# Moving two of three transposes of each matrix set from TensorE to VectorE and DRAM, for the first 20 of 32 images

## The chip, the cores and the metric

The kernel runs on one core of a Trainium2 chip. The metric is the time on the device in microseconds (us) from the start to the end of one execution. Everything is float32. The engines are TensorE (PE, with its weight loads shown apart as PEld), VectorE (DVE), ScalarE (ACT), GpSimd (POOL) and SyncE (SP), which here only issues DMAs.

## The reference, cut to what matters

The input x is 32 images of 32 channels of 128x128. Layer 0 normalizes the image in 16 groups of two channels, takes each channel's matrix X to five steps of a coupled Newton iteration for a matrix square root, and adds the result to x. Layer 1 normalizes again, takes a two-dimensional Fourier transform, keeps 64x32 modes, multiplies them by weights over the channels, transforms back and adds.

```python
def _L0_conv_ref(A):                      # A: normalized x, 1024 matrices of 128x128
    normA = jnp.sqrt(jnp.sum(A2 * A2, axis=(1, 2)))
    Y = A2 / normA[:, None, None]
    Z = I
    for _ in range(5):
        T = 0.5 * (3.0 * I - jnp.matmul(Z, Y))
        Y = jnp.matmul(Y, T)
        Z = jnp.matmul(T, Z)
    return Y * jnp.sqrt(normA)[:, None, None]

x = x + _L0_conv_ref(_gn(x))
x = x + _L1_conv_ref(_gn(x), weights1, weights2)
```

The change touches only layer 0.

## The kernel before, in words

**Sets.** The unit of work of layer 0 is a set: four channels of one image, held as a tile of 128 partitions by 4 x 128 numbers (256 KB). There are 256 sets, eight to an image. The five iterations are rewritten as polynomials: `newton` (L305) runs two `quartic` blocks (L294) and a few more products. A "group" below is one `products` (L245) or one `transposed` (L251): four 128x128 products, or four 128x128 transposes by a product with the identity, into one PSUM bank. A set takes ten groups of products and three groups of transposes: one in each `quartic` (L299, of `v`), and one of `m` (L313).

**A quartic.** PE multiplies `mb` and `m`; DVE adds `m` to the PSUM result and writes `v` (L297, through `plus`, L239). PE transposes `v`, and DVE adds `r` to it and writes `w` (L299). PE multiplies `v` and `w`, and DVE adds a multiple of the identity and writes `q` (L301). `r` is `mb` plus a multiple of the identity, made by POOL at L291 and L315. The other products are copied from PSUM by ACT (`taken`, L231).

**Staging.** `fetch` (L259) loads a set twice through ACT's DMA queue, as it is (`b`) and transposed (`xt`). `staged` (L265) normalizes both: four POOL operations make `m` from `xt` (L272), four ACT operations make `mb` in place (L282), and POOL makes `r`. The means and scales come from `prep` (L160), which loads the image once more (`xs`, L167) and runs `bn_stats` on DVE.

**What sets the order.** Every engine runs its instructions in the order in which the program issues them. The program is a loop of rounds (L783). In each round it goes over the lanes (four, `LANES`); a lane holds one `newton` generator and makes one step of it, up to the next `yield`. A quartic has three steps and the whole `newton` thirteen calls, the last of which only ends it, so the lane is then free. Lanes start three rounds apart, so that at any time four sets are at different steps, and what a step needs was issued one round before. Between the lanes one step each is made of `preps`, `specs`, `posts`, `prods` and `backs`: the statistics of the next image, the forward transform (`settle` L333, which stores the finished `xt` to `mid` through SP's queue, lets POOL fold it and DVE take `bn_stats` of it; `forward`, `spectrum`), the products over channels, and the way back (`inverse` L636). The images are in three parts of 21, 8 and 3 (`GROUPS`); products and way back of the first part start after its 21st image and run beside the Newton steps of the images after it.

**Memory.** The pool `sets` (L109) holds the sets' tiles, with a fixed number of buffers for each name (three of `v`, `w`, `q`; four of `r`, `x`, `y`; ten of `xt`; six of `b`). The pools `modes` and `inv` (L106 and L107), used only from the 21st image on, are held from the start.

Of the kernel before, what the change touches and what calls it, by code (L numbers as in the profile page):

```python
# [21 lines left out]
F32 = mybir.dt.float32  # L25
AF = mybir.ActivationFunctionType
# [6 lines left out]
B = 32  # L33
C = 32
G = 16
LANES = 4
GROUPS = (21, 8, 3)


# [2 lines left out]
QD = 39 / QA  # L42
EYE = 36 / 16
QS = EYE / QD
NB = 8
EPS = 1e-5
K = 64
# [12 lines left out]
def conv_preact_kernel(  # L60
# [42 lines left out]
    up = ctx.enter_context(tc.tile_pool(name="up", bufs=1))  # L103
    sp = ctx.enter_context(tc.tile_pool(name="sp", bufs=1))
    small = ctx.enter_context(tc.tile_pool(name="small", bufs=1))
    modes = ctx.enter_context(tc.tile_pool(name="modes", bufs=1))  # L106
    inv = ctx.enter_context(tc.tile_pool(name="inv", bufs=1))  # L107
    phase = ctx.enter_context(ExitStack())
    sets = phase.enter_context(tc.tile_pool(name="sets", bufs=1))  # L109
    ps8 = ctx.enter_context(tc.tile_pool(name="ps8", bufs=8, space=PSUM))  # L110

    diags = [modes.tile([P, 2048], F32, name=f"diag{i}") for i in range(2)]
    plain = [modes.tile([P, 1024], F32, name=f"plain{i}") for i in range(2)]

    tail = False

# [40 lines left out]
    def prep(b, made):  # L160

        st = small.tile([P, C, 6], F32, tag="a_st", name=f"a_st{b}", bufs=2)
        tiles = []

        def load(i):
            t = stp.tile([P, 4, P], F32, tag="xs", name=f"xs{b}_{i}")
            kept(nc.scalar.dma_start(out=t, in_=xt_in[b, :, 4 * i : 4 * i + 4, :]))  # L167
            tiles.append(t)

        for i in range(3):  # L170
            load(i)
        yield
        for i in range(C // 4):
            for c in range(4):
                nc.vector.bn_stats(st[:, 4 * i + c, :], tiles[i][:, c, :])  # L175
            yield
            if i + 3 < C // 4:
                load(i + 3)
        _, nm, d = yield from moments(st, "a")
        q = small.tile([P, C], F32, tag="a_qs", name=f"a_qs{b}")  # L180
        nc.vector.tensor_reduce(
            q, d.rearrange("p g (c e) -> p (g c) e", e=2), AX.X, ALU.add
        )
        yield
        pq = bank()[:, 0, 0:C]
        nc.tensor.matmul(pq, avg_mean, q, start=True, stop=True)

        v = small.tile([P, C + G], F32, tag="a_v", name=f"a_v{b}")
        nc.vector.tensor_scalar_mul(v[:, 0:C], pq, -512 / (P * P))
        yield  # L190
        vg = small.tile([P, G], F32, tag="a_vg", name=f"a_vg{b}")
        nc.vector.tensor_reduce(
            vg, v[:, 0:C].rearrange("p (g c) -> p g c", c=2), AX.X, ALU.add
        )
        nc.vector.tensor_scalar(v[:, C:], vg, 0.5, EPS, ALU.mult, ALU.add)
        s = root(v, C + G, "a_r")
        inv = small.tile([P, C + G], F32, tag="a_inv", name=f"a_inv{b}")
        nc.vector.reciprocal(inv, s)
        yield

        sc = small.tile([P, C], F32, tag="a_sc", name=f"a_sc{b}", bufs=2)
        nc.vector.tensor_scalar_mul(sc, inv[:, 0:C], 1.0 / P)
        n = small.tile([P, G, 2], F32, tag="a_n", name=f"a_n{b}")
        nc.vector.tensor_tensor(  # L204
            n,
            s[:, 0:C].rearrange("p (g c) -> p g c", c=2),
            inv[:, C:, None].to_broadcast([P, G, 2]),
            ALU.mult,
        )
        nn = small.tile([P, C], F32, tag="a_nn", name=f"a_nn{b}")  # L210
        nc.vector.tensor_scalar_mul(
            nn, n.rearrange("p g c -> p (g c)"), P * (1.5 / EYE) ** 2
        )
        sn = root(nn, C, "a_t")

        scr = small.tile([P, C], F32, tag="a_scr", name=f"a_scr{b}", bufs=2)
        nc.vector.tensor_scalar_mul(scr, sc, QR * QS)
        off = small.tile([P, G, 2], F32, tag="a_off", name=f"a_off{b}", bufs=2)
        nc.vector.tensor_tensor(
            off,  # L220
            scr.rearrange("p (g c) -> p g c", c=2),
            nm[:, :, None].to_broadcast([P, G, 2]),
            ALU.mult,
        )
        made[b] = (nm, sc, sn, scr, off.rearrange("p g c -> p (g c)"))
        yield

    def four(tag, bufs):
        return sets.tile([P, 4, P], F32, tag=tag, name=tag, bufs=bufs)

    def taken(ps, tag, bufs=4, f=1.0):  # L231
        t = four(tag, bufs)
        if f == 1.0:
            nc.scalar.copy(t, ps)  # L234
        else:
            nc.scalar.mul(t, ps, f)  # L236
        return t

    def plus(ps, f, t, tag, bufs=4):  # L239

        s = four(tag, bufs)
        nc.vector.scalar_tensor_tensor(s, ps, f, t, ALU.mult, ALU.add)  # L242
        return s

    def products(lhsT, rhs):  # L245
        ps = bank()
        for j in range(4):
            nc.tensor.matmul(ps[:, j, :], lhsT[:, j, :], rhs[:, j, :], start=True, stop=True)  # L248
        return ps

    def transposed(t):  # L251
# [5 lines left out]
    raw = {}  # L257

    def fetch(b, g):  # L259
        xt, t = four("xt", 10), four("b", 6)  # L260
        kept(nc.scalar.dma_start(out=t, in_=x[b, :, 4 * g : 4 * g + 4, :]))
        kept(nc.scalar.dma_start(out=xt, in_=xt_in[b, :, 4 * g : 4 * g + 4, :]))
        raw[b, g] = xt, t

    def staged(b, g, nm, sc, sn, scr, off):  # L265

        chans = range(4 * g, 4 * g + 4)
        m = four("x", 4)
        xt, mb = raw.pop((b, g))
        for j, c in enumerate(chans):  # L270
            kept(
                nc.gpsimd.tensor_scalar(  # L272
                    m[:, j, :],
                    xt[:, j, :],
                    nm[:, c // 2 : c // 2 + 1],
                    sc[:, c : c + 1],
                    ALU.add,
                    ALU.mult,
                )
            )  # L280
            kept(
                nc.scalar.activation(  # L282
                    mb[:, j, :],
                    mb[:, j, :],
                    AF.Identity,
                    bias=off[:, c : c + 1],
                    scale=scr[:, c : c + 1],
                )
            )
        r = four("r", 4)  # L290
        nc.gpsimd.tensor_tensor(r, mb, eye, ALU.add)  # L291
        return xt, m, mb, r

    def quartic(m, mb, r):  # L294


        v = plus(products(mb, m), -1 / (QA * QR * QS), m, "v", 3)  # L297
        yield
        w = plus(transposed(v), -QA * QS, r, "w", 3)  # L299
        yield  # L300
        q = plus(products(v, w), -QA / (16 * QS), eye, "q", 3)  # L301
        yield
        return q

    def newton(g, sn, xt, m, mb, r):  # L305


        q = yield from quartic(m, mb, r)
        y = taken(products(q, m), "y")
        yield  # L310
        m = taken(products(q, y), "m", 3)
        yield
        mb = taken(transposed(m), "mb", 2, QR * QS)  # L313
        r = four("r", 4)
        nc.gpsimd.tensor_tensor(r, mb, eye, ALU.add)  # L315
        yield
        q = yield from quartic(m, mb, r)
        pw, py = products(q, m), products(q, y)
        w, y = taken(pw, "t", 3), taken(py, "y4", 2)
        yield  # L320
        t = plus(products(w, q), -0.5 * EYE / 1.5, eye, "t", 3)
        yield
        ps = products(t, y)
        for j in range(4):
            c = 4 * g + j
            nc.vector.scalar_tensor_tensor(  # L326
                xt[:, j, :], ps[:, j, :], sn[:, c : c + 1], xt[:, j, :], ALU.mult, ALU.add
            )
        yield

    folds = {}

    def settle(b, g, st, xt):  # L333

# [7 lines left out]
            )  # L342
        for j in range(4):
            nc.vector.bn_stats(st[:, 4 * g + j, :], xt[:, j, :])
        yield

    def forward(b, q, u):
# [376 lines left out]
    late = []  # L724
    late_wts = []
    lanes = [None] * LANES
    todo = [(b, g) for b in range(B) for g in range(C // 4)]
    fetches = list(todo)
    stages = list(todo)
# [3 lines left out]
    def stage():  # L733

        b, g = stages.pop(0)
        if g == 0:
            while b not in made:
                step(preps)
            if b + 1 < B:
                preps.append(prep(b + 1, made))  # L740
        ready.append(staged(b, g, *made[b]))
        if fetches:
            fetch(*fetches.pop(0))

# [37 lines left out]
    rounds = 0  # L782
    while todo or any(lanes) or posts or specs or prods or backs:  # L783
        tail = not todo and not any(lanes)
        if tail and not posts and not late:

            phase.close()
# [2 lines left out]
                late_wts.append(late[0].tile([P, 2, 4, 4, C], F32, name=f"wt{kk}_late"))  # L790
                nc.gpsimd.dma_start(out=late_wts[-1], in_=wk[kk])
        for i in range(LANES):
            if lanes[i] is None and todo and rounds >= 3 * i:
                b, g = todo.pop(0)
                xt = ready[0][0]
                lanes[i] = (b, g, xt, newton(g, made[b][2], *ready.pop(0)))
                if stages:
                    stage()
            if lanes[i] is not None:
# [79 lines left out]
```

## Time and profile before

The page and the table describe one profiled execution. Engine times are busy times; a busy PE is one with at least one product under way.

| what | us |
|---|---|
| median of 3 runs (3231.84 to 3234.92) | 3232.51 |
| the profiled execution | 3229.76 |
| its span, first to last instruction | 3227.9 |
| PE busy in the span | 3072.5 |
| PE busy in 100 us at 2500 us, inside the second half | 89.54 |
| DVE, POOL, ACT busy in the span | 2316.4, 1767.5, 1467.4 |

The kernel has two halves. Up to about 1940 us there are Newton sets and the forward transform only; after that the way back of earlier images runs beside the Newton sets of later ones, and DMA traffic doubles. The change acts in the first of them, so shares of the whole span say less than those of the stretch from 100 to 1700 us.

### The profile page before, as it was taken

What the parts mean: (1) busy time and instruction counts of PE and PEld (TensorE: products, weight loads), DVE (VectorE), ACT (ScalarE), POOL (GpSimd) and SP (SyncE); (2) the same over time, 40 slices, a digit from 0 to 9 for tenths busy, and PEclk for the clock granted to TensorE, in tenths of its full rate; (3) what the DMA queues carried; (4) which work ended last, traced back from release to release, by engine and by line L of the source; (5) the groups of instructions that cost most, each with busy time, mean ns of one, the idle gap of its engine ahead of it and who ended that gap; (6) DMA issues with size and microseconds to landing.
All of it is one profiled execution on the core that took longest, in us unless ns stands there. A gap on an engine that the chain in (4) does not pass through costs nothing.

```text
span 3227.9 us, 78350 instructions
## 1 busy us (share of the span) xinstructions
PE 3072.5 (95%) x30656; PEld 2949.3 (91%) x30656; DVE 2316.4 (72%) x6408; ACT 1467.4 (45%) x3076; POOL 1767.5 (55%) x2312
## 2 busy tenths in 40 slices
PE   6999999999999999999999999999999899999954
PEld 6999999999999999999999999999899888989854
DVE  6777777777777777777777776578777777756646
ACT  3444444444444444444444444444444444435433
POOL 4555555455555555555555554376667667636642
PEclk9999999999999999999999999999999999999985
DMA  3333333332233333333333236766666676576577
GB/s 125 102 102 99 105 100 101 99 97 94 92 100 102 100 105 102 102 102 102 96 97 95 93 102 212 228 226 203 227 208 226 210 235 225 180 214 210 193 262 251
DMA packets 270722, 478.06 MB, mean 148 GB/s; under 512 B 80912, under 2 KB 90384, under 8 KB 270352
## 3 DMA queue, kind: packets, MB, share of 16 engines
q1 hardware_dynamic: 154864, 253.84, 24.0%
q10 hardware_dynamic: 113472, 211.86, 20.6%
q0 software_dynamic: 2016, 7.34, 0.6%
q8 instruction: 242, 3.96, 0.5%
q14 instruction: 128, 1.05, 0.1%
HBM read 319.06 MB, written 153.88 MB: 147 GB/s over the span
## 4 chain that ended last, share of the span: by engine, by line
PE 85%; DMA 6%; DVE 6%; ACT 1%; issue 1%; POOL 0%; SPq 0%; ACTq 0%; DVEq 0%; POOLq 0%
PE ps L248 67%; PE ps L254 11%; DMA xs<-in_xt 3%; PE ps L358 2%; PE ps L680 2%; DVE yt L697 2%; DMA or<-od 1%; PE ps L492 1%; PE ps L395 1%; PE ps L658 1%; DVE xt L326 1%; DVE a_st L175 1%; PE ps L563 1%; DMA od<-om 0%; DVE q L242 0%
## 5 line engine op out<-in xcount | busy, mean ns | idle before, releaser
L340 POOL TENSOR_TENSOR fold<-xt 128x256 f32<-128x256 f32 x512 | 363.3, 731 | 600.0 <-DVE xt L326 535.7
L291 POOL TENSOR_TENSOR r<-b,eye 128x512 f32<-128x512 f32 x256 | 327.2, 1278 | 638.0 <-issue 613.1
L248 PE MATMUL ps<-w,v 128*128 128x128 f32 x4096 | 550.0, 278 | 5.6 <-DVE w L242 5.5
L248 PE MATMUL ps<-y,q 128*128 128x128 f32 x4096 | 548.1, 277 | 0.3 <-ACT y L234 0.3
L248 PEld LDWEIGHTS ps<-w,v 128*128 128x128 f32 x4096 | 502.2, 193 | 8.3 <-DVE w L242 4.5
L248 PEld LDWEIGHTS ps<-y,q 128*128 128x128 f32 x4096 | 504.1, 194 | 1.3 <-ACT y L234 0.7
L234 ACT COPY y<-ps 128x512 f32<-128x512 f32 x512 | 299.8, 586 | 357.4 <-PE ps L248 356.9
L272 POOL TENSOR_SCALAR x<-xt,a_nm,a_sc 128x128 f32<-128x128 f32 x1024 | 451.9, 456 | 16.8 <-DVE a_n L204 15.8
L282 ACT ACTIVATE b<-b,a_off,a_scr 128x128 f32<-128x128 f32 x1024 | 422.4, 485 | 1.6 <-DMA b<-in_x 1.6
L242 DVE SCALAR_TENSOR_TENSOR w<-ps,r 128x512 f32<-128x512 f32 x512 | 349.9, 685 | 74.8 <-PE ps L254 70.3
L242 DVE SCALAR_TENSOR_TENSOR q<-ps,eye 128x512 f32<-128x512 f32 x512 | 348.5, 682 | 54.1 <-PE ps L248 46.7
L633 POOL TENSOR_TENSOR yt<-yt,d 128x512 f32<-128x512 f32 x236 | 298.1, 1290 | 152.4 <-ACT d L692 138.5
L242 DVE SCALAR_TENSOR_TENSOR v<-ps,m 128x512 f32<-128x512 f32 x256 | 176.4, 689 | 242.5 <-PE ps L248 242.0
L326 DVE SCALAR_TENSOR_TENSOR xt<-ps,a_t_s,xt 128x128 f32<-128x128 f32 x1024 | 289.6, 341 | 84.2 <-PE ps L248 80.8
L315 POOL TENSOR_TENSOR r<-mb,eye 128x512 f32<-128x512 f32 x256 | 326.8, 1276 | 32.8 <-ACT mb L236 32.7
L242 DVE SCALAR_TENSOR_TENSOR v<-ps,x 128x512 f32<-128x512 f32 x256 | 176.6, 690 | 219.5 <-PE ps L248 219.2
L236 ACT ACTIVATE mb<-ps 128x512 f32<-128x512 f32 x256 | 153.1, 598 | 381.4 <-PE ps L254 370.2
L254 PE MATMUL ps<-ident,v 128*128 128x128 f32 x2048 | 311.3, 275 | 7.2 <-DVE v L242 6.9
L248 PE MATMUL ps<-m,q 128*128 128x128 f32 x2048 | 285.5, 283 | 18.7 <-DVE q L242 16.1
L248 PE MATMUL ps<-y,t 128*128 128x128 f32 x2048 | 279.5, 280 | 3.5 <-DVE t L242 3.4
L248 PEld LDWEIGHTS ps<-m,q 128*128 128x128 f32 x2048 | 253.5, 195 | 28.7 <-DVE q L242 16.8
L248 PE MATMUL ps<-x,b 128*128 128x128 f32 x2048 | 273.4, 277 | 3.9 <-POOL x L272 3.9
(117 smaller groups left out, 5212.5 us busy)
## 6 DMA issues: line engine op xcount, KB each, us to landing
b<-in_x ACTq DMA_DIRECT2D x256, 256.0 KB
xt<-in_xt ACTq DMA_DIRECT2D x256, 256.0 KB
xs<-in_xt ACTq DMA_DIRECT2D x256, 256.0 KB
mid<-xt SPq DMA_DIRECT2D x256, 256.0 KB
yt<-mid SPq DMA_DIRECT2D x128, 512.0 KB
out<-yt SPq DMA_DIRECT2D x108, 512.0 KB
ob<-od SPq DMA_DIRECT2D x42, 256.0 KB
out<-yt ACTq DMA_DIRECT2D x20, 512.0 KB
```

The source lines that it names most:

```text
L234: nc.scalar.copy(t, ps)
L236: nc.scalar.mul(t, ps, f)
L242: nc.vector.scalar_tensor_tensor(s, ps, f, t, ALU.mult, ALU.add)
L248: nc.tensor.matmul(ps[:, j, :], lhsT[:, j, :], rhs[:, j, :], start=True, stop=True)
L254: nc.tensor.transpose(ps[:, j, :], t[:, j, :], ident)
L272: nc.gpsimd.tensor_scalar(m[:, j, :], xt[:, j, :], nm[:, c // 2 : c // 2 + 1], sc[:, c : c + 1], ALU.add, ALU.mult,)
L282: nc.scalar.activation(mb[:, j, :], mb[:, j, :], AF.Identity, bias=off[:, c : c + 1], scale=scr[:, c : c + 1],)
L291: nc.gpsimd.tensor_tensor(r, mb, eye, ALU.add)
L315: nc.gpsimd.tensor_tensor(r, mb, eye, ALU.add)
L326: nc.vector.scalar_tensor_tensor(xt[:, j, :], ps[:, j, :], sn[:, c : c + 1], xt[:, j, :], ALU.mult, ALU.add)
L340: nc.gpsimd.tensor_tensor(f[:, :, 64 * half : 64 * half + 64], xt[:, :, 0:64], xt[:, :, 64:128], op)
L633: engine.tensor_tensor(yh, yh, d, op)
```

## The change

For images 0 to 19 (`FIRST = GROUPS[0] - 1 = 20`), called far in the code, the transpose of `v` in both quartics is no longer made on PE. DVE transposes `v` in blocks of 32x32 into a tile `turn`; SP stores that to DRAM in rows of 2 KB and loads it back into `w` in pieces of 512 bytes, which puts the blocks where they belong; POOL then adds `r` in place. `r` is written by POOL in the same order of blocks, and PE reads `w` through a view that undoes it. The transpose of `m` stays on PE. The other 12 images keep all three transposes on PE.

So that POOL needs only an addition, the factor `-QA * QS` of L299 moves into the scale of `m` (`MS`). Two of the four normalizations of `m` move from POOL to ACT, for all images. The staging of a set is now a generator `norms`, stepped once for each lane of each round.

A far quartic has five steps in place of three (`v`, its transpose and the store; the load; nothing; the addition; the product), so a far `newton` has 17 calls where it had 13. There are six lanes, of which sets of the last 12 images use four (`LESS`); a new set starts every 17/6 rounds (far) or 13/4 rounds. The pools `modes` and `inv` are made only when 160 sets are settled; until then their place is taken by `early`, which holds the additional buffers.

```diff
-LANES = 4
+LANES, LESS = 6, 4
+FAR, NEAR = 17 / 6, 13 / 4
...
+MS = -QA * QS
+FIRST = GROUPS[0] - 1
...
+    rooms = dict(b=(6, 2), xt=(10, 4), x=(4, 2), r=(4, 3), v=(3, 3), w=(3, 3), q=(3, 1), y=(4, 2))
+    rooms.update(m=(3, 2), mb=(2, 1), t=(3, 1), y4=(2, 1), turn=(0, 3))
...
+    def blocks(t):
+        return t.rearrange("p c x -> p (c x)").rearrange("p (a c j) -> p a c j", a=4, c=4)
+
+    def plus_eye(mb, far):
+        r = four("r", far)
+        if far:
+            nc.gpsimd.tensor_tensor(
+                blocks(r).rearrange("p a c j -> p c a j"),
+                mb.rearrange("p c (a j) -> p c a j", a=4),
+                eye.rearrange("p c (a j) -> p c a j", a=4),
+                ALU.add,
+            )
+        else:
+            nc.gpsimd.tensor_tensor(r, mb, eye, ALU.add)
+        return r
...
+        for j in range(4):
+            c = 4 * g + j
+            if j < 2:
...
+            else:
+                on_scalar(m[:, j, :], xt[:, j, :], offm, sc, c)
+            on_scalar(mb[:, j, :], mb[:, j, :], off, scr, c)
+            yield
+        ready.append((xt, m, mb, plus_eye(mb, b < FIRST)))
...
-        v = plus(products(mb, m), -1 / (QA * QR * QS), m, "v", 3)
-        yield
-        w = plus(transposed(v), -QA * QS, r, "w", 3)
-        yield
-        q = plus(products(v, w), -QA / (16 * QS), eye, "q", 3)
+        v = plus(products(mb, m), -1 / (QA * QR * QS), m, "v", far)
+        if far:
+            t = four("turn", far)
+            nc.vector.transpose(blocks(t), v.rearrange("p c (i b) -> p b c i", b=4))
+            held = dram.tile([P, 512], F32, name="turn", tag="turn", bufs=8)
+            kept(nc.sync.dma_start(out=held, in_=t.rearrange("p c x -> p (c x)")))
+            yield
+            w = four("w", far)
+            kept(
+                nc.sync.dma_start(
+                    out=blocks(w).rearrange("p a c j -> p a (c j)"),
+                    in_=held.rearrange("(a i) (b x) -> (i b) a x", a=4, b=4),
+                )
+            )
+            yield
+            yield
+            nc.gpsimd.tensor_tensor(w, w, r, ALU.add)
+            w = blocks(w).rearrange("p a c j -> p c a j")
+        else:
+            yield
+            w = plus(transposed(v), 1.0, r, "w", far)
+        yield
+        q = plus(products(v, w), 1 / (16 * QS * QS), eye, "q", far)
...
+        if early and len(settled) >= FIRST * (C // 4):
+            change()
...
-            if lanes[i] is None and todo and rounds >= 3 * i:
+            step(norms)
+            far = todo and todo[0][0] < FIRST
+            room = lanes[i] is None and (far or LANES - lanes.count(None) < LESS)
+            if todo and room and rounds >= due:
+                due = max(due, rounds - 1) + (FAR if far else NEAR)
+                while norms:
+                    step(norms)
```

## The prediction, made before the changed kernel ran

> **What bounds the kernel now.** I read the page's forty slices first, to see whether one limit holds throughout. It doesn't: after slice 24 the DMA share doubles. So I cut the span into stretches; the columns are the stretch, its length, busy us of PE, PEld, DVE, ACT and POOL (instructions), granted clock, DMA share, GB/s:
>
> ```profile
> 100.00:500.00 400.00, 399.83 (x3620) 389.40 (x3619) 301.10 (x884) 184.17 (x382) 208.62 (x297) 1.00 0.31 99
> 500.00:900.00 400.00, 399.80 (x3622) 388.52 (x3622) 294.49 (x854) 185.65 (x384) 203.56 (x287) 1.00 0.32 100
> 900.00:1300.00 400.00, 399.84 (x3625) 388.78 (x3625) 300.15 (x878) 182.65 (x379) 208.25 (x295) 1.00 0.31 99
> 1300.00:1700.00 400.00, 399.80 (x3617) 389.16 (x3616) 296.24 (x863) 184.88 (x382) 204.87 (x288) 1.00 0.32 102
> ...
> 2400.00:2800.00 400.00, 372.89 (x3568) 352.58 (x3569) 306.16 (x778) 184.00 (x417) 281.99 (x324) 0.96 0.66 219
> ```
>
> In the first four PE is never without a product for more than 0.05%, while DVE is busy 74.5%, POOL 51.6%, ACT 46.1%. The chain of waits of 100 to 1700 us says the same: every step of it is PE.
>
> ```profile
> by line: PE ps L248 82.1%; PE ps L254 13.6%; PE ps L358 2.1%; PE ps L395 1.2%; PE ps L147 0.3%; PE ps L423 0.2%; PE ps L186 0.2%; PE ps L420 0.1%; PE ps L364 0.1%; PE ps L370 0.1%; issue 0.0%
> ...
> 571.43 6.33 PE ps L248 x56
> 659.63 6.33 PE ps L248 x56
> 747.83 6.33 PE ps L248 x56
> 836.03 6.33 PE ps L248 x56
> ```
>
> The same piece returns every 88.20 us: one image, so a set takes 11.03 us. L254, the transposes, is 13.6% of 1600 us, 217.6 us for 18.14 images. An image has 27 groups of transposes (24 of sets, 2 of `forward`, 1 of `spectrum`), hence 0.444 us a group. (A matmul's own row says 275 ns each; that is latency, the pitch is 111.)
>
> The rows by shape give the pieces of the change that exist (busy us, mean ns):
>
> ```profile
> L242 DVE SCALAR_TENSOR_TENSOR w<-ps,r 128x512 f32<-128x512 f32 x512 | 349.9, 685 | 74.8 <-PE ps L254 70.3 <-POOL x L272 1.7 <-issue 0.6
> L315 POOL TENSOR_TENSOR r<-mb,eye 128x512 f32<-128x512 f32 x256 | 326.8, 1276 | 32.8 <-ACT mb L236 32.7
> L272 POOL TENSOR_SCALAR x<-xt,a_nm,a_sc 128x128 f32<-128x128 f32 x1024 | 451.9, 456 | 16.8 <-DVE a_n L204 15.8 <-DMA xt<-in_xt 0.9
> L282 ACT ACTIVATE b<-b,a_off,a_scr 128x128 f32<-128x128 f32 x1024 | 422.4, 485 | 1.6 <-DMA b<-in_x 1.6
> L132 DVE TENSOR_TENSOR b_r_q<-b_r_q,b_v 128x1 f32<-128x1 f32 x32 | 25.3, 791 | 1.1
> L437 ACT ACTIVATE spec<-ps,b_inv 128x512 f32<-128x512 f32 x32 | 38.2, 1195 | 8.6 <-PE ps L254 7.5 <-DVE b_inv L432 1.1
> ```
>
> The last two are there for what they warn of.
>
> **What the Trainium skill says.** (1) "VectorE: DVE Perf Modes", The three transpose paths: DVE transposes only within 32x32 blocks, 311 ns for 128x128 in bf16; no float32 figure, and this trace has no such operation. (2) "Vector Engine (DVE) Microarchitecture Reference", 3.8: the transpose sustains one element per cycle per lane. (3) "SBUF — State Buffer", Who interferes with whom: a DVE operation with two SBUF inputs and a GpSimd operation shut each other out of a shared port. The trace agrees: L132 adds one number per partition in 791 ns mean, 159 at least. (4) "DMA: Bandwidth & Descriptors", Two DMAs through the same engine are not ordered: a load of what an earlier DMA wrote must wait for its landing. So store and load latencies add up.
>
> **The change part by part.**
>
> PE. Two groups for each of 160 sets go: 320 x 0.444 = 142 us, all on the path. An image then takes 88.20 - 7.11 = 81.09 us, a set 10.14, and a round (6/17 of a set) 3.58 us, where it was 11.03 x 4/13 = 3.39.
>
> DVE. 8.22 us a set now (74.5% of 11.03). Two `w` additions of 0.685 leave, two transposes of 128x512 come. From below: 311 ns less 128 elements at 0.96 GHz leaves 178 ns fixed, plus 512 elements: 0.71 us (estimate from pages 1 and 2; the clock is the first page's). From above: each read is 16 bytes from the last, and ACT needs 1195 ns at L437, where it writes 32 bytes apart, for what takes 586 densely, so twice per element: 1.24 us. I take 0.75: `a_ms` (L144) reads every third number of 64 in 222 ns, no slower than the dense 64 of L154 (226). DVE: 8.35 of 10.14, 82%; at 1.24 us 92%. Waits for the port like L132's grow with POOL's share, perhaps 0.3 us a set more.
>
> POOL. Two of four L272 (0.44 each) go, two additions like L315 (1.28) come: 5.69 + 1.68 = 7.37 us, 73%. The blocked order of `r` has rows of 32 numbers instead of 128; the folds (rows of 64, 731 ns for 256) lie on the same line as L315, so rows cost nothing visible. ACT gets two more of 0.41 us: 5.08 + 0.83 = 5.9, 58%. Both engines have the idle time that hides this.
>
> DMA. 1.05 MB more per set, 103 GB/s beside 109 now: 212 GB/s. The stretch after 2400 us carries 219 at a share of 0.66, so it fits. In pieces of 512 bytes the load needs about 30 ns a packet (in the trace 128 bytes take 13 ns and 2048 take 84): 1 us over 16 engines.
>
> The round trip. From PE's start on `mb` x `m` to its start on `v` x `w` there are four rounds, 14.3 us. In it: the products with their latency 1.2 (1004.38 to 1005.54 in the timeline), a wait in DVE's queue 0.5, `v` 0.69, transpose 0.75, store, load, a wait in POOL's queue 0.7, addition 1.28. `mid` stores of the same 256 KB land 2.0 us after issue (median, 200 to 1700 us; 2.5 beyond 2000 us, where DMA is as busy as it will be), the `b` and `xt` loads after 2.9 and 3.3 (3.7 and 4.2): I take 2.4 and 3.9. Sum 11.4, 2.9 under the budget; with every part at its upper end (transposes 1.24, queues 1 and 1.3, store 4.7, load 6.8: ninth deciles beyond 2000 us) 18.2. Behind the load's wait on SP stand the next lane's store and the `mid` stores. All DMAs of SP and ACT also take their landing semaphores from one set of eight in turn; with eight DMAs a set where there were four, one comes round after a set, not two, so a late store can hold up an issue on ACT, and behind it the copies of `y` and `m`.
>
> Ramp. With few lanes a round is bound by latency. PE now is full some 20 us after its first product at 25 us, having lost about 8. Six lanes fill in 15 rounds; up to round 12 I count 16 us of PE work over rounds of about 3 us (four of them must hold the 12 us trip): 23 us lost, 15 to 18 more than now. I take +17.
>
> Change-over. The first near set waits until three lanes are empty, 8.5 rounds after the last far start instead of 3.25. PE runs thin for some 12 rounds, about 2.2 us of work in 3: +8.
>
> Second half. Near sets are as before but for half of L272 on ACT, where POOL is busy 70% and ACT 46%; PE idles 27 of 400 us there for many small reasons. I take 0, between -15 and +15.
>
> Residual stalls. PE can't make up for any wait, and DVE's work bunches: calls 1, 13 and 16 fall in one round (0.69 + 0.75 + 0.69 + 1.1, plus `bn_stats` twice 1.1, 5.4 us against 3.6). 1% of 1620 us: +16, between 0 and 50.
>
> Sum against the profiled execution: 3229.8 - 142 + 17 + 8 + 16 = 3129. That execution lies 2.7 us under the median, a difference I leave out.
>
> **The rivals.**
>
> B, DVE takes half the gain. The transpose costs 1.24 us, DVE is at 92% plus its port waits and lags in every third round, so PE waits 0.4 us a set: 160 x 0.4 = 64 more, 3190. For it: reads 16 bytes apart. Against: L144.
>
> C, slower: the round trip decides. A round can't be shorter than a quarter of the trip, so a set costs 17/6 x trip / 4 = 0.708 x trip. At 14.3 us PE no longer decides; at 15.6 a set costs 11.03 us as before. With DMA at two thirds and every issue in line behind others' landings, I put this case at 16.0 us: a set costs 11.33, 160 x 0.30 = 48, plus ramp 17 and change-over 8: 3303. For it: the ninth deciles. Against: the medians. DVE alone would reach the same point only at a transpose of 2.1 us, outside my bounds.
>
> D, nothing moves: the transposes weren't what PE waited for. The chain excludes it (13.6%); only costs that happen to cancel leave it a chance.
>
> **How the numbers follow.** A has 0.48 with its own range 3085 to 3165; B 0.17; C 0.31; D 0.04. A and B are faster: 0.65. Within 0.2% (what a measurement of this kernel can't tell from no change): 0.04. Slower 0.31. The predicted time is A's, 3129. Below 3085 I leave 0.04; from C the range takes the half under 3300, leaving out some 0.15.
>
> **What would show it.** L254 at half its time; the image's pitch near 81 us; PE without gaps from 100 to 1600 us; a DVE transpose row at 0.7 to 0.8 us; POOL's addition ending before PE reaches `v` x `w`. I am wrong if PE's waits name POOL `w` or a DMA in that stretch (C), or DVE `q` and `v` (B).

## The result, and the profile after

| | median us | from, to | runs |
|---|---|---|---|
| before | 3232.2 | 3231.8 to 3234.9 | 4 |
| after | 3317.9 | 3307.4 to 3326.3 | 4 |

The change makes the kernel slower: ratio 1.0262, 95% interval 1.0226 to 1.0297, +86 us where 3129 was predicted. The profiled execution of after spans 3310.1 us.

The first view is again the busy time by stretches (stretch, length, busy us of PE, PEld, DVE, ACT, POOL, granted clock, DMA share, GB/s), for the changed kernel:

```profile
100.00:500.00 400.00, 377.20 (x3285) 361.65 (x3285) 326.90 (x862) 209.72 (x449) 261.86 (x289) 0.98 0.62 194
500.00:900.00 400.00, 374.34 (x3278) 359.30 (x3277) 327.36 (x851) 206.66 (x441) 261.05 (x289) 0.99 0.60 190
900.00:1300.00 400.00, 375.64 (x3266) 361.14 (x3265) 330.15 (x873) 207.07 (x446) 258.94 (x287) 0.98 0.62 194
1300.00:1700.00 400.00, 377.78 (x3319) 362.94 (x3319) 328.65 (x854) 211.93 (x453) 260.86 (x288) 0.99 0.61 190
...
2400.00:2800.00 400.00, 368.41 (x3566) 348.14 (x3565) 300.75 (x760) 207.57 (x472) 250.94 (x262) 0.98 0.65 214
```

PE was without work for 0.2 us of 400; now it is for some 24, and even while it works it is not at full clock: 0.98 to 0.99 where it was 1.00. It completes 3280 instructions in 400 us where it completed 3620. A set now has 8 instructions of PE fewer (two groups of four transposes; a transpose is one instruction of PE, a float32 product two), and no more sets pass than before. DVE went from 75% to 82% of the stretch, POOL is at 65%, ACT at 52%. No engine is full.

Where the time went is seen by comparing when the store of the nth finished set to `mid` is issued in the two traces (256 such stores, worked out from their issue times):

| stretch of the kernel | predicted us | measured us |
|---|---|---|
| up to set 8 (ramp) | +11 (+17, and 8 of 160 sets of -142 and +16) | +28.5 |
| sets 8 to 160 (far, steady) | -120 (152 of 160 sets of -142 and +16) | +15.5 |
| sets 160 to 168 (change-over) | +8 | +3 |
| sets 168 to 256 (near) | 0 | +33 |
| after the last set | 0 | +2.4 |

The measured rows sum to the difference of the spans, 82.2 us. The steady stretch is by far the largest miss: the transposes did leave PE there, and their 135 us did not come back as time. The page's rows by shape name what waits (busy us, mean ns, idle before it and its releaser):

```profile
L367 POOL TENSOR_TENSOR w<-w,r 128x512 f32<-128x512 f32 x320 | 407.4, 1275 | 408.7 <-DMA w<-turn 328.9
...
L297 PE MATMUL ps<-m,q 128*128 128x128 f32 x2048 | 295.2, 289 | 83.3 <-DVE q L272 82.6
L354 DVE STREAM_TRANSPOSE turn<-v 128x512 f32<-128x512 f32 x320 | 357.9, 1119 | 7.0
```

The transpose takes 1.12 us, not 0.75. POOL's addition is the row with the most idle time before it, and mostly a DMA ends it, which looks like rival C. Whether that costs anything is asked of PE, not of POOL. PE's waits between 200 and 1600 us (us in total, times, longest):

```profile
PE ps L297 <- DVE q L272: 39.9, 34, 3.9
PE ps L203 <- DVE a_qs L198: 16.1, 11, 3.2
PE ps L297 <- DVE t L272: 14.8, 20, 3.1
...
PE ps L297 <- POOL w L367: 2.4, 4, 1.8
```

PE waits for POOL's `w` 2.4 us in 1400, for DVE's `q`, `t` and `a_qs` (a step of the statistics) 70.8. By the prediction's own signs that is rival B and not C. POOL was merely early: its wait for the DMA is idle time that costs nothing as long as nobody waits for POOL. The timeline shows one of the long waits, first DVE (start, us, what):

```profile
1020.84 0.67 DVE L272 SCALAR_TENSOR_TENSOR v<-ps,m 128x512 f32<-128x512 f32 x1
1021.55 1.13 DVE L354 STREAM_TRANSPOSE turn<-v 128x512 f32<-128x512 f32 x1
1022.61 0.65 DVE L272 SCALAR_TENSOR_TENSOR v<-ps,x 128x512 f32<-128x512 f32 x1
1023.28 1.08 DVE L354 STREAM_TRANSPOSE turn<-v 128x512 f32<-128x512 f32 x1
1024.30 1.07 DVE L397 SCALAR_TENSOR_TENSOR xt<-ps,a_t_s,xt 128x128 f32<-128x128 f32 x4
1025.30 0.67 DVE L272 SCALAR_TENSOR_TENSOR q<-ps,eye 128x512 f32<-128x512 f32 x1
```

and PE behind it:

```profile
1026.03 2.07 PE L297 MATMUL ps<-m,q 128*128 128x128 f32 x8 [3.69 <-DVE q L272]
1027.90 1.92 PE L297 MATMUL ps<-y,q 128*128 128x128 f32 x8
1029.60 1.06 PE L303 MATMUL ps<-ident,m 128*128 128x128 f32 x4
1030.46 1.48 PE L297 MATMUL ps<-w,v 128*128 128x128 f32 x8
1031.78 1.06 PE L297 MATMUL ps<-x,b 128*128 128x128 f32 x8
```

PE's last product before the gap ended near 1022.3. DVE has no gap: `v`, transpose, `v`, transpose and `xt` of other sets stand ahead of the `q` that PE needs. When `q` comes, PE needs 2.07 us for a group of four products (eight instructions) instead of 1.06, and its instructions start 213 ns apart instead of 111 until some 5.3 us after the restart: about 2.6 us more are lost after the 3.69 of the gap.

### The profile page after: what moved, and what is told of

It reads as the page before. It is cut to its first block, busy times and chain, and to the rows that moved or that the text cites. A ratio compares the mean times of both kernels' runs of the same rounds, so it can differ in the third digit from the quotient of the medians.

```text
span 3310.1 us, 77971 instructions
## 1 busy us (share of the span) xinstructions
PE 3001.5 (91%) x29376; PEld 2856.1 (86%) x29376; DVE 2477.9 (75%) x6440; ACT 1664.8 (50%) x3588; POOL 1935.0 (58%) x2120
## 5 line engine op out<-in xcount | busy, mean ns | idle before, releaser
L367 POOL TENSOR_TENSOR w<-w,r 128x512 f32<-128x512 f32 x320 | 407.4, 1275 | 408.7 <-DMA w<-turn 328.9
L324 ACT ACTIVATE b<-b,a_off,a_scr 128x128 f32<-128x128 f32 x1024 | 474.0, 485 | 119.8 <-issue 66.6
L297 PEld LDWEIGHTS ps<-y,q 128*128 128x128 f32 x4096 | 513.1, 197 | 6.8 <-ACT y L266 4.9
L297 PE MATMUL ps<-m,q 128*128 128x128 f32 x2048 | 295.2, 289 | 83.3 <-DVE q L272 82.6
L354 DVE STREAM_TRANSPOSE turn<-v 128x512 f32<-128x512 f32 x320 | 357.9, 1119 | 7.0
L291 POOL TENSOR_TENSOR r<-b,eye 128x512 f32<-128x512 f32 x96 | 122.4, 1275 | 346.9 <-issue 294.5
L192 DVE BATCH_NORM_STATS2 a_st<-xs 128x6 f32<-128x128 f32 x1024 | 229.2, 278 | 109.1 <-DMA xs<-in_xt 108.8
L266 ACT ACTIVATE t<-ps 128x512 f32<-128x512 f32 x256 | 153.2, 598 | 311.9 <-PE ps L297 288.0
L297 PE MATMUL ps<-m,mb 128*128 128x128 f32 x2048 | 279.7, 280 | 18.4 <-ACT mb L266 11.6
L266 ACT ACTIVATE y<-ps 128x512 f32<-128x512 f32 x256 | 152.6, 596 | 276.2 <-PE ps L297 267.4
```

Source lines behind the costliest of these rows:

```text
L297: nc.tensor.matmul(ps[:, j, :], lhsT[:, j], rhs[:, j], start=True, stop=True)
L324: nc.scalar.activation(t, x, AF.Identity, bias=offset[:, c], scale=scale[:, c])
L354: nc.vector.transpose(blocks(t), v.rearrange("p c (i b) -> p b c i", b=4))
L367: nc.gpsimd.tensor_tensor(w, w, r, ALU.add)
```

## The experiments

"Far delay" below is the delay against before that is gained between the 8th and the 160th set (after: +15.5 us; PE's removed transposes alone would give -135). All times are medians in us, with the ratio to before and its interval.

**Which part costs: the DVE transposes, the trip, or neither.** e1_no_blocks stores `v` as it is, without the block transpose:

```diff
-            t = four("turn", far)
-            nc.vector.transpose(blocks(t), v.rearrange("p c (i b) -> p b c i", b=4))
...
-            kept(nc.sync.dma_start(out=held, in_=t.rearrange("p c x -> p (c x)")))
+            kept(nc.sync.dma_start(out=held, in_=v.rearrange("p c x -> p (c x)")))
```

> Leaves out the block transposes of DVE: v itself is stored to DRAM and loaded back into w, so w's values are not the transpose; everything else stays. Theory D (DVE's 1.12 us transposes and what queues behind them hold PE): 2.24 us of DVE work a set go, the stretch 200 to 1600 us shows PE without gaps and a set every 10.2 to 10.5 us, in all 3180 to 3230 us. Theory M (the round trip and its traffic hold PE: POOL, ACT and the loads of the statistics wait for DMAs): gaps stay, 3290 to 3330 us.

e2_no_trip writes the block transpose straight into `w` and has no DMA:

```diff
-            nc.vector.transpose(blocks(t), v.rearrange("p c (i b) -> p b c i", b=4))
...
-            kept(nc.sync.dma_start(out=held, in_=t.rearrange("p c x -> p (c x)")))
...
+            nc.vector.transpose(blocks(w), v.rearrange("p c (i b) -> p b c i", b=4))
```

> Leaves out the trip through DRAM: POOL adds r to the 32x32-transposed blocks where they lie, so the blocks are not moved to their places; the empty steps stay. Theory D: DVE is as busy as before, the time changes by less than 30 us, 3290 to 3320. Theory M: PE without gaps, 3180 to 3230 us.

e3_neither has no transposes on DVE and no DMA; the five steps stay:

```diff
-            t = four("turn", far)
-            nc.vector.transpose(blocks(t), v.rearrange("p c (i b) -> p b c i", b=4))
...
-            nc.gpsimd.tensor_tensor(w, w, r, ALU.add)
+            yield
+            yield
+            yield
+            nc.gpsimd.tensor_tensor(w, v, r, ALU.add)
```

> Leaves out both the block transposes and the trip: POOL adds r to v. Both theories: what is left is PE's own pace of 10.14 us a set, plus the longer ramp and whatever the last 96 sets lost: 3130 to 3180 us. If it stays above 3230, something else in the change (POOL's additions, the staging in small steps, six lanes) holds PE.

| kernel | median | ratio (interval) | far delay |
|---|---|---|---|
| e1, trip alone | 3252.4 | 1.0054 (1.0038 to 1.0071) | -44 |
| e2, transposes alone | 3304.4 | 1.0213 (1.0193 to 1.0233) | +6 |
| e3, neither | 3195.7 | 0.9883 (0.9866 to 0.9900) | -99 |
| after, both | 3317.9 | 1.0262 (1.0226 to 1.0297) | +15.5 |

From 200 to 1600 us (same columns as above) e3 reads

```profile
200.00:1600.00 1400.00, 1378.47 (x12359) 1332.52 (x12359) 996.08 (x2959) 785.31 (x1685) 983.59 (x1082) 1.00 0.34 105
```

and e2

```profile
200.00:1600.00 1400.00, 1317.18 (x11557) 1265.52 (x11557) 1168.07 (x3020) 735.16 (x1573) 920.76 (x1013) 0.99 0.32 98
```

The count of PE instructions is the pace. Without either part PE keeps 99 of the 135 us that the transposes gave it; the kernel stays 16 us above what was expected of it. The transposes on DVE alone add 109 us to e3, the trip alone 57, both 122, so they are not additive; that a PE kept back by one has time for the other would explain it. e1 lies between the two times that were expected, since both parts cost. In e2 nobody waits for a trip, and DVE is at 83%: the DVE part alone is enough to lose the whole gain.

**How long a transpose takes, and why.** e4_dense lets each read take neighbouring numbers (other numbers than the reference's, same amount):

```diff
-            nc.vector.transpose(blocks(t), v.rearrange("p c (i b) -> p b c i", b=4))
+            nc.vector.transpose(blocks(t), v.rearrange("p c (b i) -> p b c i", b=4))
```

> The transpose reads 32 adjacent numbers instead of every fourth one (the rows of w come out in another order, so the values differ); all other work is the same. If the reads 16 bytes apart make it slow, it falls from 1.12 to about 0.71 us, and under theory D the total falls by a third to a half of e1's gain; if float32 itself does, it stays at 1.1 us and so does the total, 3305 to 3330. Under theory M the total stays in either case.

3289.0, 1.0164 (1.0120 to 1.0209); far delay -13. Its transposes (min/median/max ns, first and last start) read

```profile
L354 DVE STREAM_TRANSPOSE turn<-v x320: 645/711/714, 28.8 to 1798.0; 128x512 f32<-128x512 f32 x160
```

and those of the changed kernel

```profile
L354 DVE STREAM_TRANSPOSE turn<-v x320: 995/1124/1216, 29.0 to 1822.7; 128x512 f32<-128x512 f32 x160
```

711 ns is the lower bound that the prediction had worked out as an estimate from two pages of the Trainium skill ("VectorE: DVE Perf Modes", The three transpose paths, and "Vector Engine (DVE) Microarchitecture Reference", 3.8: one element per cycle and lane; the fixed part is the estimate's); this run agrees with 0.71 us. Reading every fourth number costs 0.41 us more. That is 0.82 us of DVE a set, and by the medians 29 of the 65 us by which the changed kernel exceeds e1 (e4's own runs spread from 3265 to 3302). The stride is part of the transposes' cost, not the whole.

**What of the trip costs.** e9_idle_trip leaves the DMAs of e1 in place but loads them into a tile that nobody reads, and POOL adds `r` to `v`:

```diff
-            w = four("w", far)
+            dump = four("turn", far)
...
-            nc.gpsimd.tensor_tensor(w, w, r, ALU.add)
+            w = four("w", far)
+            nc.gpsimd.tensor_tensor(w, v, r, ALU.add)
```

> As e1_no_blocks (no block transposes), with every store and load of the trip still issued, but the load goes into a tile that nobody reads and POOL adds r to v directly: the trip's traffic and its places in the queues stay, no engine waits for its data. If the waits for the data cost what the trip costs (e1 against e3: 57 us), it falls to 3190 to 3210 us; if the traffic, SP's and ACT's queues and the shared landing semaphores do, it stays at 3235 to 3255.

3214.5, 0.9945 (0.9919 to 0.9972); far delay -85. By the medians the traffic as such (against e3) costs 19 us, waiting for its data (against e1) 38; e9's runs spread from 3197 to 3222. So the trip does have a price when the transposes don't hide it.

**The edits that were costed at nothing.** e5_all_near makes no set far (`FIRST = 0`), which leaves the near pace, the generator for staging and the half of `m` on ACT. e14_pacing_alone gives, in addition, `m` back to POOL (`if j < 4:`) and stages a set at once:

```diff
+        while norms:
+            step(norms)
```

> FIRST = 0: all 32 images keep their three transposes on PE and run in four lanes, with the change's other edits (half of m's normalization on ACT, staging in small steps, pacing). If these edits cost the 33 us that the changed kernel loses in its last 88 sets, this one loses them there too and ends at 3260 to 3285 us; if they were left behind by the far sets, it ends at 3225 to 3240 us.

> As e5 (no trip anywhere), and all sets are staged at once when a lane starts and normalized on POOL alone, as before the change; what is left is the pacing and the renamed scales. If the staging edits cost e5 its 33 us: 3228 to 3242 us; if the pacing does: 3260 to 3270.

e5: 3266.3, 1.0100 (1.0084 to 1.0117). e14: 3250.0, 1.0050 (1.0037 to 1.0063). With nothing moved off PE, these edits cost 32 us, of which about 16 go with the staging edits and 16 stay with what is left, the pacing by `due` above all. e5's time is the one expected if its last 88 sets lose 33 us, but they don't: it loses 12 us in the ramp and 20 between the 8th and the 160th set. e6_near_pool and e7_near_staging ask whether that is what the near sets of the changed kernel lose: e6 gives near sets all of `m` on POOL (`if j < (2 if b < FIRST else 4):`), e7 besides stages them at once.

> The changed kernel, but sets of the last 12 images normalize m on POOL alone, as before. If ACT's two more operations a set are what the second half loses, it gains 25 to 45 us on the changed kernel, 3275 to 3295; if POOL's relief there helped, it loses 5 to 20, 3320 to 3335; if it is the small steps or the pacing, no change.

> As e6, and sets of the last 12 images are staged at once when a lane starts, as before. If the small steps cost the second half, it gains 25 to 45 us on e6; if it equals e6, what is left is the pacing and the order of the lanes.

e6: 3340.3, 1.0332 (1.0317 to 1.0348); e7: 3319.0, 1.0271 (1.0246 to 1.0295). e6 is 22 us slower than the changed kernel, a little more than was expected if POOL's relief helps there, and e7 is back at its time. The last 88 sets have +46 and +29 against before, where the changed kernel has +33: neither is the cause. In e5 these sets have +0.4, in e14 +8, while e3 has +45 although its far stretch is fast. So the edits within the near sets don't cost the +33 by themselves; it comes after a far stretch. e10_phase shifts by two rounds which round the way back leaves out (`(rounds + 2) % 5`):

> The changed kernel with one number moved: the way back rests in every fifth round, and here that is the round two earlier. If the 33 us that the last 88 sets lose come from how the way back's steps fall among the sets' steps, that stretch (1369 us from the 168th set to the end) moves by more than 15 us; if not, by less than 8.

3310.9, 1.0267 (1.0232 to 1.0303). Its last 88 sets took +18 in the one profile, a change of the size that was expected if the phase matters. But the profile is of the fastest of its four runs (3296 to 3328), and its median can't be told from the changed kernel's. The cause of this term stays open.

**DVE's amount of work.** e12_less_stats makes one of the four `bn_stats` of a finished set for images 1 to 18, which frees 0.67 us of DVE a set:

```diff
-        for j in range(4):
+        for j in range(1 if 0 < b < FIRST - 1 else 4):
             nc.vector.bn_stats(st[:, 4 * g + j, :], xt[:, j, :])
```

> The changed kernel, but for images 1 to 18 only one of a set's four bn_stats of the finished xt is made (the statistics of the second normalization are incomplete): DVE has 0.67 us less a set, the trip is as it was. Theory D: it gains 15 to 40 us on the changed kernel, 3275 to 3303. If the trip's length alone holds PE: less than 8 us.

POOL clears the unused places, once an image. 3320.7, 1.0269 (1.0254 to 1.0284): no gain at all, where the theory that DVE's load is what costs expected 15 to 40 us, with DVE down from 1148 to 1085 us between 200 and 1600 us:

```profile
200.00:1600.00 1400.00, 1312.15 (x11493) 1258.99 (x11491) 1085.48 (x2641) 731.18 (x1567) 916.93 (x1022) 0.99 0.62 192
```

Compare e4: 0.82 us a set taken out of the transposes is worth 29 us, 0.67 us taken out of `bn_stats` nothing. It isn't how busy DVE is, but what is made longer: in the changed kernel's waits of PE for `q` and `t`, 54.7 us between 200 and 1600 us, DVE spends 0.1 us on `bn_stats`. It is never idle in them: half of the time is `q` and `t` themselves, 15 us the additions to `xt`, 13 us `v` and the transposes.

**The time for the trip.** e13_longer_trip adds one more empty step to the far quartic (19 calls); e8_deep loads `xs` one step earlier, with a fourth buffer.

```diff
-FAR, NEAR = 17 / 6, 13 / 4
+FAR, NEAR = 19 / 6, 13 / 4
...
             yield
             yield
+            yield
             nc.gpsimd.tensor_tensor(w, w, r, ALU.add)
```

```diff
-    stp = ctx.enter_context(tc.tile_pool(name="stp", bufs=3))
+    stp = ctx.enter_context(tc.tile_pool(name="stp", bufs=4))
...
-            if i + 3 < C // 4:
-                load(i + 3)
+            if i + 4 < C // 4:
+                load(i + 4)
```

> The changed kernel with one more empty step in each trip: 19 calls a set, a start every 19/6 rounds, so the trip may take five rounds of 3.2 us (16.0 us) instead of four of 3.58 (14.3 us). If the trip's length holds PE, it gains 25 to 60 us, 3255 to 3295; under theory D less than 10, or it loses, since every other step then has a shorter round.

> The changed kernel with four buffers instead of three for the statistics' own loads xs, which are then issued one step earlier. If DVE's waits for xs (5.5% of the chain from 200 to 1600 us) are a cause of their own, the total falls by 20 to 60 us, 3260 to 3300; if they only fill time that DVE's or PE's other waits would take, by less than 15.

e13: 3437.1, 1.0628 (1.0612 to 1.0643), far delay +148; e8: 3313.2, 1.0249 (1.0233 to 1.0264), no difference. More time for the trip makes it much worse, and the trace of e13 says why (DVE and PE):

```profile
1013.47 0.63 DVE L272 SCALAR_TENSOR_TENSOR v<-ps,m 128x512 f32<-128x512 f32 x1
...
1014.20 1.08 DVE L354 STREAM_TRANSPOSE turn<-v 128x512 f32<-128x512 f32 x1
...
1015.25 0.68 DVE L272 SCALAR_TENSOR_TENSOR v<-ps,x 128x512 f32<-128x512 f32 x1
...
1015.97 1.08 DVE L354 STREAM_TRANSPOSE turn<-v 128x512 f32<-128x512 f32 x1
1016.98 0.64 DVE L272 SCALAR_TENSOR_TENSOR t<-ps,eye 128x512 f32<-128x512 f32 x1
...
1017.67 2.07 PE L297 MATMUL ps<-y,t 128*128 128x128 f32 x8 [3.54 <-DVE t L272]
```

Its waits of PE:

```profile
PE ps L297 <- DVE t L272: 133.9, 103, 3.7
PE ps L297 <- DVE q L272: 15.7, 18, 2.3
```

With 19 calls the first `v` of one set and the second of another nearly always fall together, and `t` comes right behind them. In the order in which DVE ran its instructions, with those of the statistics left aside, `v`, transpose, `v`, transpose follow each other 154 times in e13, 146 of them with `t` next, and PE waits for `t` 103 times in 1400 us. In the changed kernel it is 73 times, 47 with `t` and 24 with `xt` and `q` next. Of its 54 waits for `q` and `t` in 1400 us, 37, and 45.5 of the 54.7 us, stand directly behind such a bunch.

**Half of the trips.** In e11_half only the first quartic takes the trip (five lanes, 15/5 rounds); e15_half_relaxed gives this 16 calls and undoes the staging edits.

```diff
-LANES, LESS = 6, 4
-FAR, NEAR = 17 / 6, 13 / 4
+LANES, LESS = 5, 4
+FAR, NEAR = 15 / 5, 13 / 4
...
-        q = yield from quartic(m, mb, r, far)
+        q = yield from quartic(m, mb, r, False)
```

> One part of the change alone: of the far sets only the first quartic takes the trip, the second keeps its transpose on PE, with 15 calls a set in five lanes (one start every three rounds). PE saves half, 71 us; DVE gets half, 0.43 us a set. If each transpose on DVE costs what it does in the changed kernel, the time lies half-way between e5 and the changed kernel, 3280 to 3300 us. If the loss comes only when DVE is nearly full (theory D), PE keeps most of its half: 3205 to 3250 us.

> As e11 (first quartic alone takes the trip, five lanes), with one more empty step for the trip and the staging as before the change. If staging costs what e5 shows and the trip's length matters: 3195 to 3230 us, faster than before; if DVE eats what PE saves in any case: 3232 to 3270.

e11: 3269.4, 1.0121 (1.0105 to 1.0138); e15: 3332.1, 1.0305 (1.0289 to 1.0321). Neither time is one that was expected. e11 is 3 us above e5, so half the trips cost what their 71 us of PE save, and this smaller dose doesn't pay either. e15, with one more step for the trip, is 63 us slower although its staging edits are undone. PE's waits in e11 and then in e15:

```profile
PE ps L297 <- DVE q L272: 25.3, 40, 1.3
PE ps L297 <- DVE t L272: 16.4, 27, 1.5
```

```profile
PE ps L297 <- DVE t L272: 62.3, 108, 2.5
```

One step more of the first quartic, and it is `t` again that comes late. These two kernels also show what a single transpose does: with one a set, two `v` with two transposes follow each other only once in each whole run. Even so 30 of e11's 42 us of waits for `q` and `t`, and all of the 62 for `t` in e15, stand directly behind a transpose (or behind the `xt` after it).

**The order on DVE.** e16_turn_last issues the transposes and their stores at the end of the round, e17_turn_xt_last the additions to `xt` too; e18_even_starts changes only the pace:

```diff
+            def turn():
+                t = four("turn", far)
...
+            late_steps.append(turn)
...
+        while late_steps:
+            late_steps.pop(0)()
```

```diff
-FAR, NEAR = 17 / 6, 13 / 4
+FAR, NEAR = 18 / 6, 13 / 4
```

> The block transposes and their stores are issued at the end of the round, behind the additions of all lanes; DVE's work, the number of DMAs and the 17 calls stay. If the order in DVE's queue is what costs (q and t stand behind a transpose of 1.1 us, and PE waits for them), PE's waits for q fall by half or more between 200 and 1600 us (from 40 us in 36 gaps) and the time falls to 3245 to 3290. If the order doesn't matter, the time is within 10 us of 3318. The trip starts later in its round, so if the trip's length decides, the time rises above 3330.

> As e16_turn_last, and the four additions that finish xt (1.1 us a set, for all images) also move to the end of the round. If the order in DVE's queue is what costs, PE's waits for q and t nearly go between 200 and 1600 us and the time is 3215 to 3275, under that of e16_turn_last. If only the transposes' place matters, it equals e16_turn_last within 10 us; if the order doesn't matter, it is within 10 us of 3318.

> The pace of far sets is 18/6 rounds instead of 17/6; the 17 calls, DVE's work and the trip's steps stay. Sets then start exactly three rounds apart, and in every round the same calls coincide: the first v and its transpose (call 1) with q and xt (13, 16), the second v and transpose (9) with t (15). At 17/6 calls 1, 9 and 15 fall in one round in most rounds (v, transpose, v, transpose, t: 4.3 us on DVE), in the one after it little. A round must then take 3.38 us instead of 3.58 for PE to be full. If it is the bunching of DVE's work that costs, PE's waits for q and t between 200 and 1600 us fall from 55 us to under 30, and the time to 3230 to 3290. If DVE's work or the trip costs whatever its phase, the waits stay and the time is 3305 to 3345; if the lesser pace itself decides (rounds no shorter than 3.58), a set costs 0.6 us more and the time rises to about 3410.

e16: 3346.2, 1.0362 (1.0330 to 1.0394). e17: 3357.2, 1.0385 (1.0349 to 1.0421). e18: 3319.9, 1.0264 (1.0245 to 1.0284). None is faster, and e16 and e17 did not make the change that they were meant to make. The description of the kernel before says that every engine runs its instructions as the program issues them. For DVE that isn't so: although the program of e16 issues the 320 transposes later, all but 32 of DVE's 6440 instructions ran in the places where they were. The compiler must have ordered them by itself; the DMAs of SP, which the code wraps in `kept` to hold their place, did move: the trip's stores come right after a `mid` store 114 times instead of 82. So e16 measured something else, the third case of its expectation: a trip that starts later. PE's waits in e16:

```profile
PE ps L297 <- DVE q L272: 37.6, 33, 4.0
PE ps L297 <- POOL w L372: 19.7, 12, 3.0
```

Those for `q` are as before, those for `w` rose from 2.4 to 19.7 us, and the time by 28. The trip has little room: medians from the transpose's start to the addition's end are 9.56 us in the changed kernel and 9.96 in e16, ninth deciles 11.3 and 12.5. e17 moved only part of what it was meant to: 342 of DVE's instructions are out of their places, where 1024 additions to `xt` and 320 transposes are issued later.

e18 did move the meeting point. PE's waits:

```profile
PE ps L297 <- DVE q L272: 52.6, 49, 3.1
PE ps L297 <- ACT mb L266: 26.2, 20, 2.7
...
PE ps L297 <- DVE t L272: 1.1, 3, 0.5
```

The waits for `t` went, as they should, and those for `q` grew by as much. DVE's order shows why: `v`, transpose, `v`, transpose is found 80 times, never with `t` behind it and 78 times with `xt` and `q`. Its edit moved the bunch and didn't break it up, so its time is the one expected if the phase doesn't matter, without telling whether the whole change would be fast in an order without such bunches. That wasn't tried; e11 and e15, which have half the transposes and no bunches, speak against it.

## Why the prediction was wrong

**PE's term was right in the main.** 0.444 us a group and a pace set by PE: e3, with the groups gone and nothing in their place on DVE and the DMA queues, gains 99 us of the 135 in sets 8 to 160. e5 shows +20 over the same sets from the other edits, which may be most of what is missing.

**The step that failed is "Residual stalls", taken at 16 us (0 to 50).** It named the mechanism, that PE can't make up for any wait and that DVE's work bunches, but sized it by guess at 1% of the stretch. Against PE's 135 us the stretch lost some 150 us, of which 36 remain in e3 without any transpose or trip. Three things were wrong in it. The calls: it bunched 1, 13 and 16; at 17/6 rounds the bunch is mostly 1, 9 and 15, two `v` with two transposes and `t`. The comparison: it set a round's work on DVE against the round, but what counts is how long one result that PE needs in the next round is kept behind others, about 4.5 us in the timeline above where `v` and transposes take 3.5 of them. The clock: a wait was priced at its length. Between 200 and 1600 us PE completes 901 instructions fewer than in e3, 100 us at e3's pace. PE's gaps are 65 us longer (86 against 21), and for the other 35 PE is busy but slower: the recorded clock is halved for 47.8 us of the 1400, which loses 24; the other 11 weren't taken apart. The Trainium skill, "TensorE: Matmul & The Clock Gate", Part 1, says that an idle window of about 3.4 us halves PE's clock until it has been busy as long. Around the 3.69 us gap the trace agrees, with half the clock for 6.8 us. But in the same trace the clock was also halved after gaps of 1.9 to 3.3 us, and not after one of 2.84, so shorter waits weren't free of it here.

That the transposes on DVE cost the gain is shown by leaving them out (e2 against e3). That it is by their place in DVE's queue is supported by the runs, not closed by them: the waits follow the bunches in number and in whom they hit (e13, e18), the transposes' length matters (e4) and that of `bn_stats` elsewhere on DVE doesn't (e12). In e11 and e15 a single transpose before `q` or `t` goes with such waits too. The whole change in an order that keeps every transpose away from `q` and `t` was not run.

**"DVE": 0.75 us a transpose.** It took 1.12, near the upper end of 1.24. The hint taken for the lower value, `a_ms`, reads 12 bytes apart and only 64 numbers; ACT's writes were the better neighbour. By e4 this term is worth about 29 us; at 0.71 us a transpose the kernel is still slower than before. Rival B named the right waits, PE's for `q`, but its price of 64 us was too small, since the transposes alone add 109 to e3, and its reason, a DVE at 92%, wasn't it: DVE is at 82%. Of the waits for the port that were feared, 0.3 us a set, the operations that had raised the fear show little: the six on L132 and L133, each made once an image, have means that sum to 2.13 us before, the same six (L149 and L150) 2.26 after.

**"The round trip": in the sum right, as a bound half right.** Store and load land after 2.7 and 3.3 us (medians between 200 and 1600 us; 2.4 and 3.9 were taken) and PE hardly waits for `w`. Rival C came closest in time (3303) and isn't what happened. But its margin was thinner than 2.9 us: e16 loses 28 us with 0.4 us more in the median and 1.2 in the ninth decile.

**"Both engines have the idle time that hides this."** POOL and ACT do (65% and 52% busy), and yet the staging and pacing edits cost 32 us where nothing is moved (e5). Their load doesn't explain that. Whether it is when a set starts and when its inputs are ready was not shown. **Ramp** 17, or 11 with what the first 8 sets were to gain, measured 28.5; **change-over** 8, measured 3.

**"Second half": 0 (-15 to +15), measured +33.** Open. It is 25 to 46 in most kernels that have a far stretch, e3 included, but 10 to 18 in e10, e13, e15 and e18, and -3 in e11; e5 and e14, without one, have 0.4 and 8.

## What to carry to other kernels

An engine at 75% isn't free capacity when another is at 100% and takes its results one step later: price new work on it by what stands behind it in its queue, and count every wait of TensorE with the slower products that may follow it. Look at the order in which the engine ran its instructions before believing that an edit moved anything. And before building a detour for work that bounds a kernel, leave the work out in a copy: e3 and its 1.2% were the most that this one could bring, in this form, even if the transposes and the trip cost nothing.

## What the runs showed of the hardware that was not expected

- A float32 block transpose of 128x512 on DVE takes 711 ns with adjacent reads and 1124 ns with reads 16 bytes apart; a `tensor_reduce` of 64 numbers with reads 12 bytes apart had shown no such cost (222 ns, where another operation on 64 adjacent numbers takes 226).
- After the gap of 3.7 us TensorE's instructions start 213 ns apart instead of 111, for some 5.3 us. In the changed kernel between 200 and 1600 us the clock was also halved after gaps of 1.9 to 3.3 us, though not after every one; gaps of up to 1.8 us left the next group at or near its pace, but for two places where one gap followed another within 2.5 us.
